# Layer norms turned by VectorE blocks and transfers instead of TensorE, in two graph attention layers

## The chip, the core and the metric

The kernel runs on one core of a Trainium2 chip. The metric is the device time of one execution in microseconds (us). The core's engines are called by the names of the profile: PE is TensorE (matmuls; PEld is its weight load, which overlaps), DVE is VectorE, ACT is ScalarE, POOL is GpSimd, and SP is SyncE, which here only issues transfers (DMAs). All data is float32.

## The reference

There are 64 graphs ("images" below) of 256 nodes with 512 features, x, and one 256 by 256 adjacency matrix. Two layers follow each other, both with a norm ahead and a residual behind:

```python
# layer 0: one head, additive attention
h = relu(layernorm(x))
h2 = h @ W                                  # 512 -> 256
e = leaky_relu(h2 @ a[0] + (h2 @ a[1]).T, 0.2) + NEG * (1 - adj)
x = x + concat([softmax(e) @ h2, h2], axis=-1)
# layer 1: eight heads of 64, masked dot-product attention
h = relu(layernorm(x))
q, k, v = (heads(h @ Wi.T + bi) for i in "qkv")
s = where(adj == 0, -inf, q @ k.T / 8)
x = x + merge(softmax(s) @ v) @ Wo.T + bo
```

A softmax without its maximum is exact as long as scores stay small. The kernel therefore bounds them from the weights' norms (the "bound check"), and at the end takes a second, slower program if the bound fails; with these inputs it does not.

## The kernel before, in words

The images are worked on in 32 groups of two (GB = 2, so GT = 4 tiles of 128 nodes each). Three groups are in flight at a time: while the attention of group g runs, the projections of group g + 1 and the first layer of group g + 2 are laid between its parts.

**The parts.** `first_layer(g)` is the whole of layer 0 and the norm of layer 1: statistics (line 340), rstd by a power on POOL (349), xn = (x - mean) * rstd on DVE (354), four 128 by 128 transposes per tile on PE into a PSUM bank pt (364), ReLU on ACT from the bank into hT (365), ph = hT by W0 (418), H copied by ACT (419), pn, the masked exponentials e, po = e by H (446), the new x and its statistics (450 to 454), and then the second norm with pt again. After it POOL makes `sums`, four sums and differences of quarters of hT (lines 376 to 379), and adds the output bias to x (470). The projections and the output product use a scheme of seven products of half-size blocks (`seven`, line 381), so that some products read hT itself and others a slice of sums: 1 and 2 read the first image's quarter of hT, 6 reads sums[1], 7 reads sums[2], 5 sums[0], 4 hT, 3 sums[3]. `project(g)` does the seven for q, k and v (21 pieces in the order 1, 2, 6, 7, 5, 4, 3), `outputs(g, b)` the seven for the output of one image, on o_sums, the same sums of oT.

**Attention.** `scores` makes sc for four heads (four PSUM banks), exponentials on ACT (572), the mask product p on DVE (573) and the sum ps on POOL (574). `weigh` of the step before makes pr (p by v) and total (line 601); DVE takes the reciprocal (604) and oT = pr * r (605).

**Order.** Everything on PE goes through `matmul` and `transpose` (lines 112 to 116, so nearly all of PE's work carries the lines 113 and 116), whose `in_order` ties each instruction to the one before it: PE's order is the program's. The other engines' orders come from the tile framework's scheduler. A group of attention has four steps; each is `weigh` of the step before, `scores`, and then pieces by a string written by hand:

```python
steps = ("uosuoosuosoosuos", "uusususususu", "uosoosuosoosuos", "uusususususu")
```

u is a piece of `project(g + 1)`, o of `outputs`, s of `first_layer(g + 2)` (which yields a GAP where it has nothing for PE). Where s finds nothing to do, a piece of the bound check, `judge()`, is run instead: it loads the weights once more in blocks of 128 columns, makes gram products and three squarings for q and k and four heads' pairs each (lines 267 to 292), and comes to a verdict.

**Buffers.** `mm` (line 90) hands out five PSUM banks in turn ("turn"): pr, sc, pt, ph, po, pn, the second bank of a projection and the second of an output product all come from it, so a bank's sixth user waits for the first one's reader. Three banks are held (`held_bank`). xn has two buffers, hT0 and hT1 two each.

**Transfers.** All are issued by SP in program order: x of group g + 3 in step two (line 125), the output of one image when its last add is done (654), the weights at the start (175, 186, 187), the check's blocks (247, 267).

**Start.** Group 0's first layer runs alone; after its second norm's first yield the constant bias b_out is made from bv by `last_bias` (lines 213 to 221: DVE makes a 128x128 tile bv, one buffer, PE multiplies, four times in turn), and the weights' sums by `weight_sums` on DVE.

Of the kernel before, what the change touches and what calls it, by code (L numbers as in the profile page):

```python
# [42 lines left out]
def bounded(  # L43
# [46 lines left out]
    def mm(name):  # L90
        return psum.tile([P, 512], F32, tag="turn", name=name, bufs=5)
# [117 lines left out]
    def last_bias():  # L209


        pb = mm("pb")
        for q in range(NQ):
            for half in range(2):
                b = small.tile([P, P], F32, tag="power", name=f"bv_{q}_{half}", bufs=1)
                nc.vector.tensor_scalar(b, ones, bv_col[:, half, q : q + 1], None, op0=ALU.mult)
                matmul(
                    pb, b, w_sb["o"][:, half, 2 * q : 2 * q + 2, :],
                    start=(q == 0 and half == 0), stop=(q == NQ - 1 and half == 1),
                )  # L220
        nc.vector.tensor_add(b_out, pb, b_out)


    def judge():
# [3 lines left out]

        part = const.tile([P, 10], F32, name="part")
        nc.vector.memset(part, 0.0)  # L230
        junk = att.tile([P, D], F32, tag="junk", name="junk", bufs=1)

        def squares(col, *srcs):
            sums = small.tile([P, HP], F32, tag="sums", name=f"sums{col}", bufs=2)
            for i, src in enumerate(srcs):
                nc.scalar.activation(
                    junk[:, : src.free_size()], src, AF.Square, accum_out=sums[:, i : i + 1]
                )
            nc.vector.reduce_sum(part[:, col : col + 1], sums[:, : len(srcs)], axis=AX.X)

        for s in range(2):
            squares(s, w0_sb[:, :, s])
        squares(2, *[w0_sb[:, c, 2:] for c in range(HP)])
        wv = att.tile([P, HP, D // HP], F32, tag="block", name="wv_block", bufs=1)
        sums = small.tile([P, HP], F32, tag="sums", name="sums3", bufs=2)
        for c in range(HP):
            nc.sync.dma_start(
                wv, wvT[:, c * P : (c + 1) * P].rearrange("(c p) o -> p c o", p=P)
            )
            nc.scalar.activation(  # L250
                junk, wv.rearrange("p c o -> p (c o)"), AF.Square, accum_out=sums[:, c : c + 1]
            )
        nc.vector.reduce_sum(part[:, 3:4], sums, axis=AX.X)
        squares(4, bcol["q"])
        squares(5, bcol["k"])
        squares(6, bv_col.rearrange("p h q -> p (h q)"))
        nc.vector.reduce_max(part[:, 7:8], bad.rearrange("p a t -> p (a t)"), axis=AX.X)
        yield
        heads = const.tile([P, P], F32, name="heads")
        nc.vector.memset(heads, 0.0)  # L260
        for j in range(2):
            nc.vector.memset(heads[j * DH : (j + 1) * DH, j * DH : (j + 1) * DH], 1.0)
        rowsq = const.tile([P, 2, HP], F32, name="rowsq")
        for n, (name, src) in enumerate((("q", wqT), ("k", wkT))):
            for hp in range(HP):
                w = att.tile([P, HP, P], F32, tag="block", name=f"w{name}_block{hp}", bufs=1)
                nc.sync.dma_start(
                    w, src[:, hp * P : (hp + 1) * P].rearrange("(c p) o -> p c o", p=P)
                )
                yield  # L270
                gram = mm(f"gram_{name}{hp}")[:, :P]
                for c in range(HP):
                    matmul(
                        gram, w[:, c, :], w[:, c, :], start=(c == 0), stop=(c == HP - 1)
                    )
                a = small.tile([P, P], F32, tag="power", name=f"power_{name}{hp}_0", bufs=1)
                nc.vector.tensor_mul(a, gram, heads)
                yield
                for i in range(3):
                    square = mm(f"square_{name}{hp}_{i}")[:, :P]  # L280
                    matmul(square, a, a, start=True, stop=True)
                    if i < 2:
                        a = small.tile(
                            [P, P], F32, tag="power", name=f"power_{name}{hp}_{i + 1}", bufs=1
                        )
                        nc.vector.tensor_copy(a, square)
                    else:
                        nc.scalar.activation(
                            junk[:, :P], square, AF.Square, accum_out=rowsq[:, n, hp : hp + 1]
                        )  # L290
                    yield
        nc.vector.reduce_sum(part[:, 8:10], rowsq, axis=AX.X)
        total = mm("total")[:, :10]
        matmul(total, ones, part, start=True, stop=True)
        norm = const.tile([P, 10], F32, name="norm")
# [44 lines left out]
        nc.vector.bn_stats(st, src[:, t, :])  # L340
        nc.vector.bn_aggr(mv[:, t, :], st)

    def norm_T(src, mv, name):


        ve = small.tile([P, GT], F32, tag="ve", name=f"ve{name}")
        nc.vector.tensor_scalar(ve, mv[:, :, 1], EPS, None, op0=ALU.add)
        rstd = small.tile([P, GT], F32, tag="rstd", name=f"rstd{name}")
        nc.gpsimd.tensor_tensor(rstd, ve, rexp, op=ALU.pow)
        xn = {}  # L350

        def normed(t):
            xn[t] = att.tile([P, D], F32, tag="xn", name=f"xn{name}_{t}", bufs=2)
            latest[0] = nc.vector.tensor_scalar(  # L354
                xn[t], src[:, t, :], mv[:, t, 0:1], rstd[:, t : t + 1],
                op0=ALU.subtract, op1=ALU.mult,
            ).ins.name

        def put(t, dst):
            if t + 1 < GT:  # L360
                normed(t + 1)
            pt = mm(f"pt{name}_{t}").rearrange("p (c t) -> p c t", c=HP)
            for c in range(HP):
                transpose(pt[:, c, :], xn[t][:, c * P : (c + 1) * P], ident)
            nc.scalar.activation(dst, pt, AF.Relu)  # L365

        normed(0)
        return put

    def halves(t, k):  # L370

        return [t[:, 2 * c : 2 * c + 2, r * k : (r + 1) * k] for r in range(2) for c in range(2)]

    def operand_sums(quads, sums):
        a11, a12, a21, a22 = quads
# [19 lines left out]

    def first_layer(g):

        xt = xs[g]
        mv = small.tile([P, GT, 2], F32, tag="mv", name=f"mv0_{g}")
        for t in range(GT):  # L400
            stats(mv, xt, t, f"0_{g}")
        put = norm_T(xt, mv, f"0_{g}")
        yield GAP

        H = big.tile([P, GT, F1 + 3], F32, tag="H", name=f"H_{g}", bufs=1)
        nc.gpsimd.memset(H[:, :, F1 + 2 :], 1.0)
        hT = {}
        for t in range(GT + 1):
            if t < GT:
                hT[t] = big.tile([P, HP, P], F32, tag="hT0", name=f"hT0_{g}_{t}")  # L410
                put(t, hT[t])
                yield
            if t == 0:
                continue
            t -= 1
            ph = mm(f"ph_{g}_{t}")[:, : F1 + 2]
            for c in range(HP):
                matmul(ph, hT[t][:, c, :], w0_sb[:, c, :], start=(c == 0), stop=(c == HP - 1))
            nc.scalar.copy(H[:, t, : F1 + 2], ph)  # L419
            nc.gpsimd.tensor_add(xt[:, t, F1:], H[:, t, 2 : F1 + 2], xt[:, t, F1:])  # L420
            yield

        pn = mm(f"pn_{g}")
# [17 lines left out]
        for r in range(GT):  # L441
# [11 lines left out]
            )  # L453
            stats(mv, xt, r, f"1_{g}")
            yield
        put = norm_T(xt, mv, f"1_{g}")
        yield GAP
        hT = big.tile([P, HP, TOK], F32, tag="hT1", name=f"hT1_{g}")
        for t in range(GT):
            put(t, hT[:, :, t * P : (t + 1) * P])  # L460
            if t == GT - 1:
                break
            yield
        sums = big.tile([P, 4, 2, N], F32, tag="sums", name=f"sums_{g}", bufs=1)
        quads = halves(hT, N)
        operand_sums(quads, sums)
        operands[g] = seven(quads, sums)

# [141 lines left out]

    def outputs(g, b):
        xt, oT = xs[g], oTs.pop((g, b))
        quads = halves(oT, P)
        sums = big.tile([P, 4, 2, P], F32, tag="o_sums", name=f"o_sums_{g}_{b}", bufs=1)
        operand_sums(quads, sums)
        ops = seven(quads, sums)
# [44 lines left out]
        for _ in part:  # L661
            pass

    gaps = 0
    for part in first_layer(0):
        gaps += part is GAP
        if part is GAP and gaps == 3:
            last_bias()
            weight_sums("q")
    short = first_layer(1) if NG > 1 else none  # L670
    for i, _ in enumerate(project(0)):
        if i % 7 == 1:
            weight_sums("kvo"[i // 7])
        next(short, None)
    run(short)
    verdict = judge()

    steps = ("uosuoosuosoosuos", "uusususususu", "uosoosuosoosuos", "uusususususu")
    waiting, late = None, none
    for g in range(NG):  # L680
        projected = project(g + 1) if g + 1 < NG else none
        short = first_layer(g + 2) if g + 2 < NG else none
        for step, parts in enumerate(steps):
# [8 lines left out]
            for part in parts:  # L692
                if part == "u":
                    next(projected, None)
                elif part == "o":
                    next(late, None)
                elif next(short, GAP) is GAP:
                    next(verdict, None)
        run(projected)
        run(short)  # L700
    weigh(*waiting)
    run(outputs(*waiting[:2]))
    run(verdict)


@with_exitstack
# [367 lines left out]
```

## Time and profile before

| what | us |
|---|---|
| median of 3 runs (lowest, highest) | 2699.2 (2699.19, 2699.45) |
| profiled execution: time | 2699.08 |
| profiled execution: span of the program on the core | 2697.3 |
| PE busy in the span | 2620.4 |
| DVE busy | 1669.7 |
| POOL busy | 1230.0 |
| ACT busy | 835.9 |
| PE, 4 transposes of a tile (pt) in the chain | 0.44 |
| DVE, xn 128x512, mean | 0.893 |
| ACT, ReLU from pt 128x512, mean | 0.599 |
| granted PE clock, mean over the run | 0.993 |

The profile is that of one execution. Its page gives busy shares, a chain of work followed back from the last instruction (who released whom), groups of instructions by line with their mean duration and the idle time of the engine ahead of them, and the transfers. The trace behind it can be asked for the instructions of an engine in order of time (timeline), for the same chain in a stretch (critical), and for busy times and the granted clock by stretches (windows). In a timeline a row is start, duration, engine, line, operation, names, and in brackets how long the engine sat idle before it and what ended that.

### The profile page before, as it was taken

What the parts mean: (1) busy time and instruction counts of PE and PEld (TensorE: products, weight loads), DVE (VectorE), ACT (ScalarE), POOL (GpSimd) and SP (SyncE); (2) the same over time, 40 slices, a digit from 0 to 9 for tenths busy, and PEclk for the clock granted to TensorE, in tenths of its full rate; (3) what the DMA queues carried; (4) which work ended last, traced back from release to release, by engine and by line L of the source; (5) the groups of instructions that cost most, each with busy time, mean ns of one, the idle gap of its engine ahead of it and who ended that gap; (6) DMA issues with size and microseconds to landing.
All of it is one profiled execution on the core that took longest, in us unless ns stands there. A gap on an engine that the chain in (4) does not pass through costs nothing.

```text
span 2697.3 us, 41512 instructions
## 1 busy us (share of the span) xinstructions
PE 2620.4 (97%) x17150; PEld 2118.8 (79%) x17150; DVE 1669.7 (62%) x2558; ACT 835.9 (31%) x1771; POOL 1230.0 (46%) x1004
## 2 busy tenths in 40 slices
PE   5999999999999999999999999999999999999997
PEld 3888888878888887887788888788878878878874
DVE  5666566666557665566665576665576656666544
ACT  2333232333332333323333323333333333233321
POOL 2353355443445443545434454435455335445343
PEclk8999999999999999999999999999999999999998
DMA  5000101000001010000000000000000000000000
GB/s 164 1 12 32 36 24 36 13 32 32 28 32 36 9 36 32 24 32 9 32 32 24 32 32 9 32 32 24 32 32 9 32 32 24 32 17 23 17 16 25
DMA packets 45890, 78.49 MB, mean 29 GB/s; under 512 B 3712, under 2 KB 10624, under 8 KB 45696
## 3 DMA queue, kind: packets, MB, share of 16 engines
q1 hardware_dynamic: 45696, 75.77, 8.1%
q8 instruction: 137, 2.24, 0.3%
q14 instruction: 57, 0.47, 0.1%
HBM read 42.21 MB, written 33.55 MB: 28 GB/s over the span
## 4 chain that ended last, share of the span: by engine, by line
PE 89%; DVE 8%; POOL 1%; issue 1%; DMA 0%; ACT 0%; DVEq 0%
PE pq L113 15%; PE pv L113 14%; PE py L113 13%; PE pk L113 13%; PE pr L113 9%; PE ph L113 8%; PE sc L113 7%; PE po L113 4%; PE pt L116 4%; DVE p L573 3%; DVE r L604 2%; PE total L113 2%; DVE k L544 1%; DVE oT L605 1%; PE pn L116 1%
## 5 line engine op out<-in xcount | busy, mean ns | idle before, releaser
L573 DVE TENSOR_TENSOR p<-p,maskT 128x1024 f32<-128x1024 f32 x256 | 398.6, 1588 | 0.6 <-ACT p L572 0.5
L572 ACT ACTIVATE p<-sc 128x512 f32<-128x512 f32 x512 | 264.4, 602 | 380.9 <-PE sc L113 380.9
L574 POOL TENSOR_TENSOR ps<-p 128x512 f32<-128x512 f32 x256 | 366.2, 1447 | 0.0
L628 DVE TENSOR_TENSOR x<-py,x 128x256 f32<-128x256 f32 x448 | 187.6, 419 | 272.8 <-PE py L113 266.9
L604 DVE RECIPROCAL r<-total 128x256 f32<-128x256 f32 x128 | 224.5, 1754 | 194.6 <-PE total L113 194.6
L113 PE MATMUL py<-wo_sb,o_sums 128*128 128x256 f32 x1024 | 266.5, 384 | 26.4 <-DVE x L628 21.6
L420 POOL TENSOR_TENSOR x<-H,x 128x256 f32<-128x256 f32 x128 | 87.7, 685 | 443.0 <-ACT H L419 441.9
L113 PE MATMUL pr<-p,v 128*32 128x256 f32 x4096 | 251.8, 385 | 5.8 <-DVE p L573 5.8
L113 PE MATMUL sc<-q,k 64*128 64x256 f32 x2048 | 255.7, 389 | 0.0
L113 PE MATMUL pq<-sums,wq_sb 128*128 128x256 f32 x1024 | 246.7, 384 | 4.2 <-POOL sums L377 3.7
L113 PE MATMUL ph<-w_sb,hT 128*128 128x258 f32 x1024 | 246.1, 383 | 0.0
L113 PE MATMUL pk<-sums,wk_sb 128*128 128x256 f32 x1024 | 244.8, 382 | 0.0
L113 PE MATMUL pv<-wv_sb,sums 128*128 128x256 f32 x1024 | 242.0, 379 | 0.1
L113 PEld LDWEIGHTS sc<-q,k 64*128 64x128 f32 x2048 | 187.2, 186 | 69.7 <-issue 52.6
L113 PEld LDWEIGHTS py<-wo_sb,o_sums 128*128 128x128 f32 x1024 | 191.2, 192 | 62.9 <-POOL o_sums L377 37.6
L365 ACT ACTIVATE hT<-pt 128x512 f32<-128x512 f32 x256 | 153.1, 599 | 266.0 <-PE pt L116 265.7
L354 DVE TENSOR_SCALAR xn<-x,mv,rstd 128x512 f32<-128x512 f32 x256 | 225.8, 893 | 9.5 <-PE pt L116 4.9
L376 POOL TENSOR_TENSOR o_sums<-oT 128x256 f32<-128x256 f32 x64 | 106.2, 1660 | 262.6 <-DVE oT L605 262.6
L113 PEld LDWEIGHTS pq<-sums,wq_sb 128*128 128x128 f32 x1024 | 190.1, 191 | 39.1 <-issue 9.9
L113 PEld LDWEIGHTS ph<-w_sb,hT 128*128 128x128 f32 x1024 | 195.7, 192 | 28.6
L113 PEld LDWEIGHTS pk<-sums,wk_sb 128*128 128x128 f32 x1024 | 189.3, 190 | 33.9 <-issue 9.9
L113 PEld LDWEIGHTS pr<-p,v 128*32 128x32 f32 x4096 | 121.1, 110 | 112.2 <-issue 39.7
(145 smaller groups left out, 4054.4 us busy)
## 6 DMA issues: line engine op xcount, KB each, us to landing
x<-in_x_dram SPq DMA_DIRECT2D x32, 1024.0 KB, 5.5
out_dram<-x SPq DMA_DIRECT2D x64, 512.0 KB, 2.8
wq_sb<-in_L_gnn_Wq_dram SPq DMA_DIRECT2D x2, 512.0 KB, 11.7
wk_sb<-in_L_gnn_Wk_dram SPq DMA_DIRECT2D x2, 512.0 KB, 12.4
wv_sb<-in_L_gnn_Wv_dram SPq DMA_DIRECT2D x2, 512.0 KB, 11.4
wo_sb<-in_L_gnn_Wo_dram SPq DMA_DIRECT2D x8, 128.0 KB, 3.3
wv_block<-in_L_gnn_Wv_dram SPq DMA_DIRECT2D x4, 256.0 KB, 3.0
wq_block<-in_L_gnn_Wq_dram SPq DMA_DIRECT2D x4, 256.0 KB, 2.9
```

Source lines behind the costliest of these rows:

```text
L113: in_order(nc.tensor.matmul(*args, **kwargs))
L116: in_order(nc.tensor.transpose(*args))
L354: latest[0] = nc.vector.tensor_scalar(xn[t], src[:, t, :], mv[:, t, 0:1], rstd[:, t : t + 1], op0=ALU.subtract, op1=ALU.mult,).ins.name
L365: nc.scalar.activation(dst, pt, AF.Relu)
L376: nc.gpsimd.tensor_add(sums[:, 0], a21, a22)
L420: nc.gpsimd.tensor_add(xt[:, t, F1:], H[:, t, 2 : F1 + 2], xt[:, t, F1:])
L544: nc.vector.tensor_add(part(1, 1), first, p7)
L572: nc.scalar.activation(pair[:, j], sc[j], AF.Exp, scale=scale)
L573: nc.vector.tensor_mul(pair, pair, maskT[:, None, :, :].to_broadcast([P, 2, NT, N]))
L574: nc.gpsimd.tensor_add(ps[:, 2 * i : 2 * i + 2, :], pair[:, :, 0, :], pair[:, :, 1, :])
L604: nc.vector.reciprocal(r, total)
L628: nc.vector.tensor_add(to, out, to)
```

## The change

For every group but the first (`by_pe` is false), a norm is no longer turned by PE. ACT applies the ReLU to xn in place; DVE's own transpose turns each tile in 32 by 32 blocks into xt, within the 32 partitions that a block lies in; and 16 transfers per image, each of 32 partitions and 256 pieces of 128 bytes, move the blocks from partitions 32i to partitions 32j of hT. xt has one buffer for all uses. hT0 is now one tile per image and not per 128 nodes, hT1 has the image as its outer dimension, and the pieces of `first_layer` are laid out anew: two tiles of xn, then an image turned and two more tiles, then the other image turned, two yields with nothing, then the products. Nineteen yields stand where there were twenty.

The bound check takes its gram products from the weights already in SBUF, four pairs of heads in one bank at a time, and runs in the pieces of group 0's first layer and projections; nothing of it is left in the main loop. The check's blocks are not loaded any more. `last_bias` makes its four bv tiles on POOL in one buffer of their own, without waiting for PE in between.

```diff
@@ last_bias
         pb = mm("pb")
+        b = att.tile([P, 2, 2, P], F32, tag="xt", name="bv_wide", bufs=1)
         for q in range(NQ):
             for half in range(2):
-                b = small.tile([P, P], F32, tag="power", name=f"bv_{q}_{half}", bufs=1)
-                nc.vector.tensor_scalar(b, ones, bv_col[:, half, q : q + 1], None, op0=ALU.mult)
+                nc.gpsimd.tensor_scalar(
+                    b[:, half, q, :], ones, bv_col[:, half, q : q + 1], None, op0=ALU.mult
+                )
...
@@ judge
+        for n, name in enumerate(("q", "k")):
+            gram = bank(f"gram_{name}")
+            for hp in range(HP):
+                half, cols = hp // 2, slice(hp % 2 * P, (hp % 2 + 1) * P)
+                for c in range(HP):
+                    w = w_sb[name][:, c % 2, c // 2 * 2 + half, cols]
+                    matmul(gram[:, hp, :], w, w, start=(c == 0), stop=(c == HP - 1))
...
+        for i in range(3):
+            for n, name in enumerate(("q", "k")):
+                square = bank(f"square_{name}{i}")
+                for hp in range(HP):
+                    a = power[name][:, hp, :]
+                    matmul(square[:, hp, :], a, a, start=True, stop=True)
...
@@ norm_T
-    def norm_T(src, mv, name):
+    def norm_T(src, mv, name, by_pe):
...
             ).ins.name
-
-        def put(t, dst):
-            if t + 1 < GT:
-                normed(t + 1)
-            pt = mm(f"pt{name}_{t}").rearrange("p (c t) -> p c t", c=HP)
-            for c in range(HP):
-                transpose(pt[:, c, :], xn[t][:, c * P : (c + 1) * P], ident)
-            nc.scalar.activation(dst, pt, AF.Relu)
...
+            if not by_pe:
+                nc.scalar.activation(xn[t], xn[t], AF.Relu)
+
+        def turned(b, dst):
+            if by_pe:
...
+                return
+
+            J = P // S
+            xt = att.tile([P, J, HP, NT, S], F32, tag="xt", name=f"xt{name}_{b}", bufs=1)
+            for t in range(NT):
+                nc.vector.transpose(
+                    xt[:, :, :, t, :], xn[b * NT + t].rearrange("p (c j a) -> p j c a", c=HP, a=S)
+                )
+            for i in range(J):
+                for j in range(J):
+                    to = dst[j * S : (j + 1) * S, :, :].rearrange("a c (t i n) -> a c t i n", t=NT, n=S)
+                    nc.sync.dma_start(
+                        to[:, :, :, i, :], xt[i * S : (i + 1) * S, j]
+                    )
...
@@ first_layer
+        by_pe = g == 0
...
+        hT = [big.tile([P, HP, N], F32, tag="hT0", name=f"hT0_{g}_{b}") for b in range(GB)]
+        normed(0)
+        normed(1)
+        yield GAP
+        turned(0, hT[0])
+        normed(2)
+        normed(3)
+        yield GAP
+        turned(1, hT[1])
+        yield GAP
+        yield GAP
+        for r in range(GT):
+            b, t = divmod(r, NT)
+            ph = mm(f"ph_{g}_{r}")[:, : F1 + 2]
...
-        put = norm_T(xt, mv, f"1_{g}")
+        normed, turned = norm_T(xt, mv, f"1_{g}", by_pe)
+        normed(0)
+        normed(1)
         yield GAP
-        hT = big.tile([P, HP, TOK], F32, tag="hT1", name=f"hT1_{g}")
-        for t in range(GT):
-            put(t, hT[:, :, t * P : (t + 1) * P])
-            if t == GT - 1:
-                break
-            yield
+        hT = big.tile([P, GB, HP, N], F32, tag="hT1", name=f"hT1_{g}")
+        turned(0, hT[:, 0])
+        normed(2)
+        normed(3)
+        yield GAP
+        turned(1, hT[:, 1])
+        yield GAP
+        yield GAP
         sums = big.tile([P, 4, 2, N], F32, tag="sums", name=f"sums_{g}", bufs=1)
...
@@ bounded, the start
-    gaps = 0
-    for part in first_layer(0):
-        gaps += part is GAP
-        if part is GAP and gaps == 3:
+    verdict = judge()
+    for piece, _ in enumerate(first_layer(0)):
+        if piece == 8:
+            next(verdict)
+        if piece == 13:
             last_bias()
+            next(verdict)
+        if piece == 15:
             weight_sums("q")
...
         next(short, None)
+        next(verdict, None)
+    run(verdict)
     run(short)
-    verdict = judge()
...
@@ bounded, the loop
-                elif next(short, GAP) is GAP:
-                    next(verdict, None)
+                else:
+                    next(short, None)
```

In the changed kernel's own numbering the ReLU is line 355, DVE's transpose 370, the transfers 376, the sums 384 to 387, the reciprocal 623 and oT 624.

## The prediction

> **What bounds the kernel now.** I read the page first: busy shares, then the chain that ended last.
>
> ```profile
> span 2697.3 us, 41512 instructions
> ...
> PE 2620.4 (97%) x17150; PEld 2118.8 (79%) x17150; DVE 1669.7 (62%) x2558; ACT 835.9 (31%) x1771; POOL 1230.0 (46%) x1004
> ...
> PE 89%; DVE 8%; POOL 1%; issue 1%; DMA 0%; ACT 0%; DVEq 0%
> ```
>
> TensorE is the bound: only 77 us of the span is without it. So a matmul removed shortens the run, and a wait put in front of one lengthens it by its full size, for line 105 (in_order) fixes TensorE's order by hand. The chain of two steps in the middle of the run gives the size of both.
>
> ```profile
> 1073.97 1.86 PE pr L113 x32
> 1075.84 0.43 PE total L113 x8
> 1076.27 1.93 PE sc L113 x16
> ...
> 1083.80 0.44 PE pt L116 x4
> ...
> 1098.61 0.86 PE py L113 x4
> 1099.47 1.73 PE pq L113 x8
> ```
>
> The columns are start, length, what. A step opens with pr, total and sc (4.22 us); then come projection products (1.73), output products (0.86) and, as pt, the norm's transposes: 0.44 us per tile. The pr of 1010.4 and 1092.5 open the same step of two groups: a group takes 82 us.
>
> **What is removed.** Each of groups 1 to 31 loses 8 tiles of pt: 8 x 0.44 = 3.5 us of TensorE per group. The bound check's 32 gram products and 24 squares, two passes each at 0.11 us (square_k: two passes in 0.22), leave the main loop: 112 x 0.11 = 12 us.
>
> **What is added.** Per tile a 32 by 32 transpose on VectorE (T), behind a ReLU on ScalarE that before read PSUM (0.60, hidden: ScalarE is 31% busy). Per image 16 transfers on SP, in a row; one buffer xt, so the next image's T waits for all 16. No row shows T. Nearest are VectorE's one-input 128x512 instructions: 0.41 (line 151) below, and 1.75 above, the reciprocal (line 604), the slowest pass. I take 0.69, what copy, reduction and statistics of that shape take.
>
> The page "VectorE: DVE Perf Modes" of the Trainium skill (The three transpose paths) gives VectorE 311 ns for 128x128 in bf16, by estimate 1.24 us for T, and its rules send a full 128x128 transpose to TensorE; no run here shows T yet. With 1.24 the sum below would rise by 33 us.
>
> For the transfers, SP's own rows at the start, 32 partitions each:
>
> ```profile
> 25.04 0.43 SPq L186 DMA_DIRECT2D wo_sb<-in_L_gnn_Wo_dram  x1
> 25.51 0.42 SPq L187 DMA_DIRECT2D bv_col<-in_L_gnn_bv_dram  x1
> ```
>
> The pitch is 0.47 us and small ones land 2.2 to 2.4 us after issue, so a set of 16 takes 15 x 0.47 + 2.3 = 9.4 us. Bounds: 0.35 and 2.2 give 7.5; 0.55 and wo_sb's 3.3 give 11.6 (the pitch of 1.36 before 24 us belongs to waits for 512 KB transfers). Pieces of 128 bytes should not bind: the 1,024 four-byte pieces of the q and k biases ran in about 1.5 us, so 256 need 0.4.
>
> The page "DMA: Bandwidth & Descriptors" (Rules for kernel authors) says that transfers under 64 KB pay mostly overhead and should be merged; its fit for GpSimd's transfers (Anatomy of one DMA), 2.0 us plus bytes over 436 GB/s, would make 16 of 32 KB one by one 33 us. The rows above overlap them instead.
>
> **First new wait: last step of a group, 1.9 us.** The order of the changed kernel's instructions shows what stands on VectorE ahead of oT (line 605), which frees pr's bank; five banks turn, pr and four sc take all, and the second v product takes pr's. Count from the step's pr. The last po ends at -2.6 (a projection and an output product now follow it). Then ri, x, three statistics and the small ones 3.2 (rows from 1074.01 on), to 0.6; rstd on POOL 1.0; xn 0.55, xn beside POOL 1.2, statistics 0.66: 4.1. T, reciprocal 1.75, T, oT 0.69 end at 7.9. The product was due at 4.22 + 1.92 = 6.1 (before, oT ended at 5.2): it waits until 8.0. The step is then 8.0 + 6 x 1.73 = 18.4 long. T at 0.41 makes the wait 1.3; T at 1.75 makes it 4.0.
>
> **Second new wait: next group's first step, 5.8 us.** The third q product needs sums (line 377). Before, POOL made sums ahead of o_sums:
>
> ```profile
> 1092.61 1.28 POOL L376 TENSOR_TENSOR sums<-hT 128x512 f32<-128x512 f32 x1 [1.41 <-PE pv L113]
> ...
> 1095.08 1.27 POOL L377 TENSOR_TENSOR sums<-sums,hT 128x512 f32<-128x512 f32 x1
> ...
> 1097.66 1.70 POOL L376 TENSOR_TENSOR o_sums<-oT 128x256 f32<-128x256 f32 x1
> ...
> 1101.80 2.50 POOL L574 TENSOR_TENSOR ps<-p 128x512 f32<-128x512 f32 x2
> ```
>
> After, POOL's order is o_sums (three), ps (two), then sums in the order 376, 378, 377. On VectorE: reciprocal 2.35 to 4.1, xn 0.55, oT to 5.4. On POOL, by the groups' means: 1.66 + 1.58 + 0.73, 2 x 1.45, 1.28 + 1.30 + 1.31 = 10.7, so line 377 is done at 16.2. TensorE is there at 4.22 + 1.92 + 0.86 + 1.73 + 1.73 = 10.4. Wait: 5.8.
>
> Are the transfers later than POOL? The last step's first image: T done at 7.2, landed 16.6. Its second image's T stands behind the sixth v product's add (17.4): done 18.8, landed 28.2, which is 9.8 in the next step; POOL comes to it at 12.3. Hidden, with 2.5 us to spare. The next group's first image: T after the third py add, 12.3, landed 21.7; ph is due at 24.8. Second image: landed 36.4, due 37.9. So at 9.4 us per set no transfer is waited for in the loop; from 11 on it is.
>
> **Third: the clock.** This trace has the same wait once, at the start:
>
> ```profile
> 63.66 3.40 PE L113 MATMUL pq<-sums,wq_sb 128*128 128x256 f32 x8 [3.69 <-POOL sums L377]
> ...
> 67.33 1.89 PE L113 MATMUL pq<-sums,wq_sb 128*128 128x256 f32 x8
> ```
>
> After 3.7 us of idling, the granted clock from 63.2 to 66.4 was 0.50, and the product took 3.40, where the next took 1.89 (1.73 in the chain, which leaves out the overlap of neighbours). A wait of 2.17 us (to 105.75) had full speed behind it. So the 5.8 us wait costs 1.7 more; the 1.9 us one does not.
>
> **Sum.** Per group 1.9 + 5.8 + 1.7 - 3.5 = 5.9 us. The step pair stands 30 times (groups 2 to 31 are prepared in the loop): +177. The check: -12. The start: bv on POOL lets pb follow po at once, not after 8.5 us and three more waits for VectorE: about -10; group 1's pt -3.5; its transfers lie beside little work: about 4 us before each image's ph, and from its last po to its first sums some 31 us (two sets 18.8, T and statistics 8, sums 4) over 18 us of products, 13 of wait: together +7. The profiled execution took 2699.1 (span 2697.3 and 1.8 around it), the median of the runs is 2699.2: 2699 + 177 - 12 + 7 = 2871; I forecast 2870. Costed at nothing: VectorE's added 8 T per group (5.5 us of 82, at 62% busy), covered except where counted; were TensorE never to wait, nothing of it would show.
>
> **Rivals.** (a) The transfers and POOL hide after all: only -3.5 per group, -105 - 12 + 7, 2590. For it: POOL is idle over half the time. Against: POOL's order, and a wait of 3.7 us in all per group already eats the gain. (b) Transfers set the pace: with 12 us per set, T waits for the set ahead of it, sums are ready at 18.1 and the fourth set 1.1 late: +3.0 per group, 2960; with 16 us every T holds VectorE up, about 29 per group, over 3500. It decides from 11 us per set. For it: 2,000 transfers of 128-byte runs, SBUF to SBUF, of which there is no row. (c) T costs 1.75: the first wait becomes 4.0, over the idling (3.1 to 3.7) that halved the clock in this trace: +3.8 per group, 2985. (d) Slower than the point of balance only by a little: POOL's chain runs shorter and the clock holds, 2.5 per group less, 2795.
>
> **Chances.** Forecast with its neighbours (2790 to 2940) 0.60, (b) 0.16, (c) 0.12, (a) 0.08, between (a) and no change 0.04. Range 2760 to 3010: it takes in T from 0.41 (2853) to 1.75 (2985), a set from 7.5 (2870) to 11.6 (2950), and (d); left out are (a) and the far part of (b). Measurement tells 0.2% (5 us) from no change: faster 0.09, same 0.03, slower 0.88.
>
> **What would show it.** In the profile after: about 250 us of idle TensorE instead of 77, most of it before pq<-sums with POOL sums as releaser, some 60 before pv with VectorE's oT; half clock in every group; T near 0.7; hT's transfers landing within 2.5 us of issue. The forecast is wrong if pq<-sums does not wait, if ph waits for a DMA, or if T is over 1.2.

## The result, and the profile after

The changed kernel takes 2985.0 us (median of 4 runs, 2980.3 to 2987.3) against 2699.3 for the kernel before (4 runs, 2699.2 to 2699.5): the ratio is 1.106, with a 95% interval of 1.104 to 1.108. The direction was forecast, and the range of 2760 to 3010 holds the time. The forecast itself, 2870, is 115 us short: 171 us more were expected, 286 came.

First the page of the changed kernel: span, busy shares, the chain that ended last by engine, then the one row of the transfers (KB each, us from issue to landing).

```profile
span 2985.7 us, 42596 instructions
...
PE 2625.0 (88%) x16158; PEld 2071.3 (69%) x16158; DVE 1822.7 (61%) x2783; ACT 842.8 (28%) x1759; POOL 1237.0 (41%) x1008
...
PE 49%; SPq 23%; DVE 13%; DMA 5%; POOL 4%; issue 4%; ACT 1%; DVEq 0%; POOLq 0%; ACTq 0%
...
hT<-xt SPq DMA_DIRECT2D x1984, 32.0 KB, 2.0
```

TensorE is busy for about as long as before although 992 matmul rows are gone, and it is now idle for 361 us of the span and not 77 (the rows of pq, ph, pv and py that stand behind waits took longer; see the clock below). In the chain, SP's queue (SPq) and the transfers (DMA) hold 28%, where DMA had 0% and SPq no entry. Below is who TensorE waits for (us in all, times, longest). pq, pk and pv are the projection products of q, k and v, py is the output product, and kept_v is ScalarE's copy of a v product out of its bank, behind which the next product adds to that bank:

```profile
PE pq L113 <- POOL sums L385: 207.7, 31, 13.6
PE pv L113 <- ACT kept_v L533: 58.4, 29, 2.3
PE ph L113 <- DMA hT<-xt: 23.6, 22, 5.8
...
PE pq L113 <- DMA hT<-xt: 4.8, 1, 4.8
```

The two waits that were forecast are there, 6.5 us per group before the third q product (207.7 less the start's 13.6, over 30) and 2.0 before a v product. A third one, ph for a transfer, was not to come. The cause of the smaller one is not the forecast's either: pv waits for kept_v, a copy on ScalarE, and not for VectorE's oT.

One group's rows in the timeline show how they hang together (start, length, engine, line, what; in brackets the idle time and what ended it). The last step of the group opens with pr at 1113.73, the next group's first with pr at 1132.51.

```profile
1119.83 37.92 SPq L376 DMA_DIRECT2D hT<-xt  x48
...
1124.57 0.63 ACT L355 ACTIVATE xn<-xn 128x512 f32<-128x512 f32 x1 [3.99 <-DVE xn L350]
...
1125.97 0.63 ACT L355 ACTIVATE xn<-xn 128x512 f32<-128x512 f32 x1 [0.78 <-DVE xn L350]
1126.51 1.05 ACT L533 COPY kept_v<-pv 128x512 f32<-128x512 f32 x2
...
1127.13 1.99 PE L113 MATMUL pv<-wv_sb,sums 128*128 128x256 f32 x8 [2.00 <-ACT kept_v L533]
...
1132.70 1.30 DVE L370 STREAM_TRANSPOSE xt<-xn 128x512 f32<-128x512 f32 x2 [1.12 <-DMA hT<-xt]
...
1141.82 2.49 POOL L593 TENSOR_TENSOR ps<-p 128x512 f32<-128x512 f32 x2
...
1145.99 1.30 DVE L370 STREAM_TRANSPOSE xt<-xn 128x512 f32<-128x512 f32 x2 [2.49 <-DMA hT<-xt]
1146.02 1.27 POOL L384 TENSOR_TENSOR sums<-hT 128x512 f32<-128x512 f32 x1 [1.71 <-DMA hT<-xt]
...
1149.97 3.77 PE L113 MATMUL pq<-sums,wq_sb 128*128 128x256 f32 x8 [6.93 <-POOL sums L385]
```

SP is taken by three sets in a row from 1119.83 to 1157.75, each held up only by the landing of the one before and the T behind it: the second image's T (1132.70) waits for the first set, the next group's T (1145.99) for the second. The second set runs from T's end, 1134.00, to 1145.99: **12.0 us**. POOL is through with ps at 1144.31 and then waits 1.7 us more, for that set. ScalarE's row shows the smaller wait: kept_v stands behind two ReLUs that wait for xn.

The granted clock around it (us, PE busy, PEld, DVE, ACT, POOL, PEclk, DMA share, GB/s):

```profile
1142.90:1149.90 7.00, 0.14 (x1) 0.00 (x0) 4.33 (x5) 0.63 (x1) 5.29 (x5) 0.78 0.19 29
1149.90:1153.40 3.50, 3.43 (x8) 2.80 (x9) 0.30 (x1) 0.63 (x1) 1.34 (x2) 0.50 0.35 54
```

The clock falls to half within the idle 7 us and stays there for the whole product behind it: 3.77 us where the next one took 1.89.

### The profile page after: what moved, and what is told of

It reads as the page before. It is cut to its first block, busy times and chain, and to the rows that moved or that the text cites. A ratio compares the mean times of both kernels' runs of the same rounds, so it can differ in the third digit from the quotient of the medians.

```text
span 2985.7 us, 42596 instructions
## 1 busy us (share of the span) xinstructions
PE 2625.0 (88%) x16158; PEld 2071.3 (69%) x16158; DVE 1822.7 (61%) x2783; ACT 842.8 (28%) x1759; POOL 1237.0 (41%) x1008
## 4 chain that ended last, share of the span: by engine, by line
PE 49%; SPq 23%; DVE 13%; DMA 5%; POOL 4%; issue 4%; ACT 1%; DVEq 0%; POOLq 0%; ACTq 0%
SPq L376 23%; PE pk L113 11%; PE py L113 9%; PE pq L113 8%; PE ph L113 7%; DMA hT<-xt 5%; PE pr L113 4%; PE po L113 4%; PE sc L113 3%; DVE xt L370 3%; DVE st L335 3%; DVE r L623 2%; DVE xn L350 2%; PE pv L113 2%; POOL rstd L345 1%
## 5 line engine op out<-in xcount | busy, mean ns | idle before, releaser
L113 PE MATMUL pq<-sums,wq_sb 128*128 128x256 f32 x1024 | 303.0, 448 | 210.3 <-POOL sums L385 207.7
L113 PEld LDWEIGHTS pq<-sums,wq_sb 128*128 128x128 f32 x1024 | 223.0, 224 | 269.1 <-POOL sums L385 222.3
L593 POOL TENSOR_TENSOR ps<-p 128x512 f32<-128x512 f32 x256 | 388.1, 1536 | 2.9 <-DVE p L592 2.9
L592 DVE TENSOR_TENSOR p<-p,maskT 128x1024 f32<-128x1024 f32 x256 | 368.0, 1469 | 2.8 <-ACT p L591 2.7
L384 POOL TENSOR_TENSOR o_sums<-oT 128x256 f32<-128x256 f32 x64 | 103.8, 1623 | 582.0 <-DVE oT L624 582.0
L355 ACT ACTIVATE xn<-xn 128x512 f32<-128x512 f32 x248 | 152.6, 628 | 539.5 <-DVE xn L350 537.4
L113 PE MATMUL pv<-wv_sb,sums 128*128 128x256 f32 x1024 | 246.5, 390 | 60.6 <-ACT kept_v L533 58.4
L113 PE MATMUL ph<-w_sb,hT 128*128 128x258 f32 x1024 | 253.2, 391 | 38.6 <-DMA hT<-xt 23.6
L113 PE MATMUL py<-wo_sb,o_sums 128*128 128x256 f32 x1024 | 278.3, 403 | 5.1 <-POOL o_sums L385 4.2
L113 PEld LDWEIGHTS pv<-wv_sb,sums 128*128 128x128 f32 x1024 | 195.5, 193 | 98.8 <-ACT kept_v L533 70.0
L350 DVE TENSOR_SCALAR xn<-x,mv,rstd 128x512 f32<-128x512 f32 x256 | 244.5, 985 | 24.3 <-POOL rstd L345 23.5
L113 PEld LDWEIGHTS py<-wo_sb,o_sums 128*128 128x128 f32 x1024 | 209.0, 207 | 51.0 <-issue 10.6
L370 DVE STREAM_TRANSPOSE xt<-xn 128x512 f32<-128x512 f32 x248 | 163.2, 686 | 108.7 <-DMA hT<-xt 107.6
```

The source lines that it names most:

```text
L113: in_order(nc.tensor.matmul(*args, **kwargs))
L350: latest[0] = nc.vector.tensor_scalar(xn[t], src[:, t, :], mv[:, t, 0:1], rstd[:, t : t + 1], op0=ALU.subtract, op1=ALU.mult,).ins.name
L355: nc.scalar.activation(xn[t], xn[t], AF.Relu)
L370: nc.vector.transpose(xt[:, :, :, t, :], xn[b * NT + t].rearrange("p (c j a) -> p j c a", c=HP, a=S))
L384: nc.gpsimd.tensor_add(sums[:, 0], a21, a22)
L592: nc.vector.tensor_mul(pair, pair, maskT[:, None, :, :].to_broadcast([P, 2, NT, N]))
```

## The experiments

All kernels below are the changed kernel with the edit shown. "First pr" is the loop's first pr, one step into it (before: 127.0), "group" the mean distance of the groups' first pr over the first 29 groups (before: 82.0, of which some 0.5 is the check's products), "sums" the median time from the pr of a group's last step to the first of the next group's sums on POOL; all three are worked out from the traces.

| kernel | us | ratio to before (95%) | first pr | group | sums |
|---|---|---|---|---|---|
| changed kernel | 2985.0 | 1.106 (1.104 to 1.108) | 168.5 | 90.2 | 32.5 |
| pe_norms | 2673.9 | 0.991 (0.989 to 0.992) | 136.1 | 80.8 | |
| layer0_blocks | 2654.1 | 0.983 (0.982 to 0.985) | 148.4 | 79.7 | |
| layer1_blocks | 2944.7 | 1.092 (1.090 to 1.093) | 154.6 | 89.2 | 32.4 |
| two_queues | 2849.8 | 1.056 (1.054 to 1.058) | 146.0 | 86.4 | 23.8 |
| sums_first | 3111.8 | 1.153 (1.151 to 1.154) | 168.1 | 94.3 | 32.2 |
| runs_1k | 2920.8 | 1.082 (1.080 to 1.083) | 158.5 | 88.4 | 26.2 |
| four_transfers | 2681.9 | 0.994 (0.992 to 0.995) | 140.4 | 81.0 | 20.6 |
| relu_on_dve | 3085.5 | 1.142 (1.139 to 1.144) | 171.6 | 93.6 | |
| relu_after_kept | 2987.3 | 1.106 (1.104 to 1.108) | 170.0 | 90.3 | 32.4 |
| four_relu | 2691.8 | 0.997 (0.996 to 0.998) | 138.4 | 81.3 | |
| layer0_late | 2646.7 | 0.980 (0.979 to 0.981) | 138.8 | 79.8 | |
| three_sets | 2716.0 | 1.006 (1.005 to 1.007) | 137.1 | 82.3 | |

### Which norm, and what is left without blocks

pe_norms:

```diff
-        by_pe = g == 0
+        by_pe = True
```

> All norms are turned by TensorE again; the new layout of pieces, the bound check in the first group and bv on POOL stay. Theory 1 (the whole loss comes from the blocks and their transfers; the check's products are moved, not removed, and what leaves the main loop, 12 us, is paid at the start): 2699 - 13 + 12, so 2690 to 2705, with the first pr at 137 to 142 us instead of 127.0. Theory 2 (the forecast's own costing: the products cost nothing at the start, and pb follows po at once): 2699 - 12 - 10 = 2677. Theory 3 (the new layout of pieces itself costs): above 2715.

layer0_blocks gives True to layer 1's `norm_T`, layer1_blocks to layer 0's:

```diff
-        normed, turned = norm_T(xt, mv, f"1_{g}", by_pe)
+        normed, turned = norm_T(xt, mv, f"1_{g}", True)
```

> Blocks in layer 0's norm alone, layer 1's norm on TensorE. Theory 1 (the wait belongs to layer 1's second set, which sums wait for; two sets of 12.4 us per group lie well inside 82 us): no pq<-sums wait in the loop, four pt of 0.44 us saved in each of 31 groups, 55 us less than the kernel with all norms on TensorE, so 2640 to 2660, with some 10 us of ph waits at the start. Theory 2 (the load of 4 T on VectorE, 4 ReLU on ScalarE and 32 transfers slows the group wherever it is put): about half of the loss stays, 2800 to 2850.

> Blocks in layer 1's norm alone, layer 0's norm on TensorE. Theory 1 (the wait before pq<-sums, 6.9 us and a half-speed product, belongs to layer 1's two sets alone): it stays as it is, ph no longer waits, 1.76 us of pt come back per group: 2960 to 3010. Theory 2 (the four sets of a group queue up on SP behind each other, so that half as many sets wait much less): the wait falls below 3.5 us and the time to 2800 to 2870.

pe_norms took 2674, below what theory 1 gave and close to the forecast's own costing, but not for the forecast's reasons: its start is 9 us longer, not 10 shorter, and a group is 0.7 us shorter than before's later groups (81.5), which neither the forecast nor the three theories had. Before, TensorE waited 21.6 us in 27 output products for VectorE's x; with the new layout that wait is down to 0.8. So the new layout, with the check and bv moved, is worth 25 us of gain; the whole loss, 311 us against pe_norms, is the blocks'.

Layer 0's blocks gain: 2654, 20 less than pe_norms though their start is 12 us longer. Layer 1's alone take 2945, somewhat below theory 1's 2960: the wait before pq<-sums stays (188.6 us in 31 times). The loss belongs to layer 1's norm: its blocks alone cost 271 us against pe_norms, layer 0's alone gain 20, and both together cost 311. So some 60 us come only when both are there; three sets in a row on SP and ph's waits in the loop are seen in that case alone.

### POOL's order, or the transfers?

The forecast laid the large wait to POOL's order (o_sums and ps ahead of sums); the rows above suggest that the transfers were no earlier. sums_first turns POOL's order round:

```diff
...
+        of = operand_sums(quads, sums)
+        if b == GB - 1:
+            for o_sum in (of[0], of[2]):
+                after(o_sum, made[0])
```

Here made[0] is the last of the next group's four sums, and the two o_sums of the second image that read oT alone are put behind it.

> POOL is made to take the next group's four sums ahead of o_sums and ps, all else as in the changed kernel. Theory 1 (the transfers set the pace: the second set lands 13.5 us after the step's pr, sums are done at 17.4 whatever stands ahead of them): the sums come no earlier, o_sums come after them, at about 22, and the output product that stands before the third q product on TensorE waits for them: about 5 us more per group, 3100 to 3170. Theory 2 (the forecast's: POOL's order makes the wait, since o_sums and ps stand ahead of sums for 7.6 us): 2 to 5 us less per group, 2830 to 2920.

Theory 1 holds, with 3112 us. The waits of TensorE in this kernel:

```profile
PE py L113 <- POOL o_sums L386: 352.6, 32, 12.6
...
PE pq L113 <- POOL sums L386: 12.8, 1, 12.8
```

The sums began 32.2 us after the last step's pr, in the changed kernel 32.5: with POOL's o_sums and ps out of their way they came no sooner. Only o_sums came later, and the output product took over the wait.

two_queues lets ScalarE issue every second transfer:

```diff
-                    nc.sync.dma_start(
+                    (nc.sync, nc.scalar)[j % 2].dma_start(
```

> The 16 transfers of a set are issued half by SP and half by ScalarE, the rest as in the changed kernel. Theory 1 (SP's pitch of 0.655 us sets the pace of a set): a set takes about 7.5 us instead of 12.4, T no longer waits for the set before, POOL starts sums when ps is done, 1.7 us earlier, ph does not wait, the start is 10 to 15 us shorter: 2880 to 2920. Theory 2 (the data movement of 128-byte pieces sets the pace): a set stays at 12 us and the time at 2975 to 2995. Theory 3 (the eight issues on ScalarE stand in front of exponentials and copies): ACT p or kept becomes a releaser of waits of TensorE and the time is above 2990.

2850 us is a larger gain than theory 1 gave. A set takes 7.5 us from its first issue to its last landing, where it took 11.8 (medians), sums come 8.7 us sooner, the start is 22 us shorter. TensorE's waits here:

```profile
PE py L113 <- POOL o_sums L385: 68.4, 18, 5.0
PE pv L113 <- ACT kept_v L533: 60.4, 58, 2.9
...
PE pq L113 <- POOL sums L385: 7.3, 1, 7.3
```

The wait before pq<-sums is gone but for the start. The median pitch of both queues is 0.66 us, so what was halved is issuing, not moving. POOL's order changed with it, sums now ahead of o_sums, which by itself (sums_first) had made the kernel slower. No run has short sets and the changed kernel's order on POOL, so what the short sets would gain without the new order is not shown. The Trainium skill, page "DMA: Bandwidth & Descriptors" (Rules for kernel authors), says that spreading transfers over several engines does not help bandwidth and only saves the issuing engine's time; the run agrees, and here that time, with POOL's new order, was worth 135 us. Theory 3 was partly right too: kept_v and copies on ScalarE stand behind the issues, and 60 us of waiting for kept_v are left.

### What a transfer costs SP

runs_1k writes each partition's kilobyte as one run, four_transfers moves a set in 4 transfers of 128 KB:

```diff
# runs_1k
...
+                    to = dst[j * S : (j + 1) * S, :, :].rearrange("a c n -> a (c n)")
+                    run = HP * NT * S
...
+                    nc.sync.dma_start(
+                        to[:, i * run : (i + 1) * run],
+                        xt[i * S : (i + 1) * S, j].rearrange("a c t n -> a (c t n)"),
+                    )
...
# four_transfers
...
+                nc.sync.dma_start(
+                    dst[i * S : (i + 1) * S, :, :].rearrange("a c n -> a (c n)"),
+                    xt[i * S : (i + 1) * S].rearrange("a j c t n -> a (j c t n)"),
+                )
```

> The same 16 transfers of 32 KB per set, from the same partitions to the same partitions, but each partition's kilobyte is written as one run and not as eight of 128 bytes; the blocks then stand at other columns of hT than the products read them from, so the output isn't the reference's. The scheduler lays ps between the sums on POOL here. Theory 1 (an issue costs SP the same whatever it describes): pitch 0.65 us, a set 12.4, 2970 to 3000. Theory 2 (the cost grows with the 256 runs of a transfer): pitch 0.47 or less as in the rows of the weights, a set at 9.5 or less, the wait before pq<-sums shorter by 3 us or more, 2860 to 2920.

> The same bytes of a set in 4 transfers of 128 KB, from 32 partitions to the same 32 partitions, one run of 4 KB per partition; the blocks are not moved across partitions, so the output isn't the reference's. POOL's order here has sums ahead of o_sums. Theory 1 (SP's pitch times the number of transfers is the set's time): a set 3 x 0.65 + 3 = 5 us, no wait before pq<-sums of over 1 us and none of ph in the loop, the two waits of 3.5 us per group and the half clock gone, 2640 to 2700. Theory 2 (what a set moves sets its time): a set above 10 us and a time above 2900. Theory 3 (T, the ReLU and the new order cost by themselves): sets short but the time above 2750.

The median issue is 0.609 us with 256 runs of 128 bytes, 0.589 with 32 runs of a kilobyte, and 0.589 with 32 runs of 4 KB and four times the bytes; with the gap behind it, 0.653, 0.633 and 0.634. In these three shapes an issue from SBUF to SBUF costs SP 0.6 us, whatever it describes. That the memories make the difference from the forecast's rows is not shown: in the changed kernel a load of x out of DRAM, issued 0.04 us behind a set (at 269.73), took 0.60 too, and 0.39 in two_queues, where SP had been idle before it (at 237.68). For the pitch theory 1 holds; for the time of runs_1k neither does: 2921 us lies between the two, at the edge of theory 2's range. The scheduler gave POOL another order in it, part of the sums ahead of o_sums, and sums began at 26.2; so of this run only the pitch is used.

With four transfers the waits for transfers are gone but for the start. In its rows for T and for the transfers T sits idle 3.0 us in all, where it was 108.7:

```profile
L370 DVE STREAM_TRANSPOSE xt<-xn 128x512 f32<-128x512 f32 x248 | 163.7, 679 | 3.0 <-DMA hT<-xt 2.9
```

```profile
hT<-xt SPq DMA_DIRECT2D x496, 128.0 KB, 2.4
```

The same bytes in a quarter of the issues take 2682 and not 2985; POOL's new order and the runs of 4 KB are part of that step, and the moves across partitions are left out. That is the page's rule on small transfers (same page and section: merge what is under 64 KB), which the forecast had weighed and set aside; the 33 us for a set that it worked out from the page's fit were too dear (12.0 measured), the rule's direction was right.

### The smaller wait

relu_on_dve moves the ReLU to VectorE:

```diff
-                nc.scalar.activation(xn[t], xn[t], AF.Relu)
+                nc.vector.tensor_scalar_max(xn[t], xn[t], 0.0)
```

> The ReLU of a tile runs on VectorE instead of ScalarE, all else as in the changed kernel. Theory 1 (the wait of 2.0 us before pv<-sums comes from ScalarE, where two ReLUs that wait for VectorE stand ahead of kept_v; and SP's three sets in a row set the end): that wait falls below 0.7 us, the wait before pq<-sums grows by as much, 2970 to 3000. Theory 2 (the forecast's: the bank is freed late by oT, behind T on VectorE): the wait before pv grows by 0.5 to 1 us, 2990 to 3030. Theory 3 (each wait adds on its own): 2985 - 29 x 2, 2925 to 2940.

3085 us lies above all three theories. The ReLU took 1.2 us a tile on VectorE, and the last v product then waited 146.8 us in 31 times for VectorE's own v. It shows that VectorE has no room for 1.2 us more per tile in that step, and leaves the question open. relu_after_kept asks it without adding work:

```diff
-            if not by_pe:
+            if not by_pe and not (name[0] == "1" and t >= NT):
...
+                if name[0] == "1" and b == 1:
+                    relu = nc.scalar.activation(xn[b * NT + t], xn[b * NT + t], AF.Relu)
+                    if kept_v[0]:
+                        after(relu, kept_v[0])
...
+                    kept_v[0] = nc.scalar.copy(to, bank).ins.name
```

> In layer 1's norm the ReLUs of the second image's two tiles are put behind the copy kept_v of the third v product on ScalarE (before, they stood ahead of it, waiting for xn from VectorE); the rest as in the changed kernel. Theory 1 (these two ReLUs make the 2.0 us wait before pv<-sums; and the three sets in a row, which begin with the first image's T, set when sums are ready): the wait before pv falls below 0.5 us, the one before pq<-sums grows from 6.6 to about 8.5 us, the time stays at 2970 to 3000. Theory 2 (each wait adds on its own): the wait before pv falls, the other stays, 2985 - 30 x 2 to 2.5, 2910 to 2930. Theory 3 (the forecast's: oT behind T frees the bank late): the wait before pv stays near 2 us.

Theory 1 holds in both halves. Groups of TensorE (busy, mean ns, idle before and its releaser), first in the changed kernel, then in this one:

```profile
L113 PE MATMUL pq<-sums,wq_sb 128*128 128x256 f32 x1024 | 303.0, 448 | 210.3 <-POOL sums L385 207.7
...
L113 PE MATMUL pv<-wv_sb,sums 128*128 128x256 f32 x1024 | 246.5, 390 | 60.6 <-ACT kept_v L533 58.4
```

```profile
L113 PE MATMUL pq<-sums,wq_sb 128*128 128x256 f32 x1024 | 303.6, 449 | 262.3 <-POOL sums L389 259.6
...
L113 PE MATMUL pv<-wv_sb,sums 128*128 128x256 f32 x1024 | 233.1, 381 | 2.2 <-DVE v L568 2.2
```

The wait before pv<-sums fell from 60.6 to 2.2 us (8.2 us of waiting for kept_v came up before pv<-hT, 0.3 each), the wait before pq<-sums rose from 210.3 to 262.3, and the time is unchanged. The two are not two costs that add up: the second ends when the transfers end, 32.4 us after the last step's pr, however TensorE spends the time until then.

> The 4 transfers of 128 KB per set that move no block across partitions (the output isn't the reference's), and the order of the ReLUs of relu_after_kept. Without the transfers' wait, removing the wait of 2.0 us before pv<-sums should now count in full: 2682 - 30 x 2.0 to 2.7 (its half clock too), 2600 to 2625. If instead it moves on to another wait as in the changed kernel, the time stays above 2665.

four_relu is four_transfers with that same order, and no faster: 2692, so the wait moved on, the second of the two cases. kept_v's wait fell from 58.0 to 8.4 us, but 57.8 us came up before the last v product, for VectorE's v. In one group's timeline the add that frees that bank (VectorE's v, 1174.49) stands behind two T and two xn, which begin at 1172.35. So even without transfers' waits VectorE's queue holds that step; whether another order there would free it was not tried.

### A version that beats both

```diff
-        by_pe = g == 0
+        by_pe = g <= 1
...
-        normed, turned = norm_T(xt, mv, f"1_{g}", by_pe)
+        normed, turned = norm_T(xt, mv, f"1_{g}", True)
```

> Blocks in layer 0's norm alone and from group 2 on; group 1's norms, which lie at the start beside little work, are on TensorE like group 0's. Theory 1 (the start's extra 12.3 us of the kernel with layer 0's blocks belong to group 1's transfers; the loop's gain stays): 2654 - 12, 2638 to 2646, faster than both kernels. If the 12 us come from something else at the start: 2650 to 2658.

2646.7, 0.7 us above theory 1's range (lowest run 2640.6) and 2.0% faster than before (interval 1.9 to 2.2). Of the 53 us some 25 are already in pe_norms; the blocks of layer 0 give the other 27, 1.0%. Most of layer0_blocks' extra start is gone: first pr at 138.8 and not 148.4. ph waits for transfers 2.6 us in all and pq for none; TensorE is at 97% again:

```profile
PE 2575.9 (97%) x16670; PEld 2063.0 (78%) x16670; DVE 1680.8 (64%) x2655; ACT 834.7 (32%) x1759; POOL 1239.6 (47%) x1008
```

three_sets has the first image of layer 1 turned by blocks as well (`by_pe` as a list per image: `[g <= 1, g <= 1]` in layer 0, `[g <= 1, True]` in layer 1).

> As layer0_late, and the first image of layer 1's norm turned by blocks too, the second by TensorE: three sets per group. Theory 1 (what hurts in layer 1 is the second set, queued behind the first; the first alone lands some 18 us after the last step's pr, about when the next step begins): two more pt per group saved, 0.88 x 30 = 26 us less than layer0_late if sums are in time, 2612 to 2622; at most 1 us per group of wait before pq<-sums, so up to 2645. If a single set in front of sums is already too late, a wait of 3 us or more and its half clock come back: above 2740.

2716 us is neither case. The sums are in time (pq<-sums idles 0.7 us in all), so a single set is not too late. But the step that prepares it is 2.5 us longer, for pt now waits for xn, and a v product for kept_v:

```profile
1177.66 0.63 PE L116 MATMUL pt<-ident,xn 128*128 128x128 f32 x4 [1.21 <-DVE xn L350]
1178.98 0.66 PE L116 MATMUL pt<-ident,xn 128*128 128x128 f32 x4 [0.69 <-DVE xn L350]
...
1184.76 1.99 PE L113 MATMUL pv<-wv_sb,hT 128*128 128x256 f32 x8 [1.67 <-ACT kept_v L533]
```

The first wait is for VectorE's queue. The second is that of the changed kernel: in ScalarE's rows kept_v (1184.14) stands behind two ReLUs (1183.08) that waited for xn. The order of relu_after_kept was not tried here.

## Why the prediction was right in direction and short in size

Per group (the groups after the check's, 81.5 us, against 90.2 now: +8.7 measured, +5.9 forecast) and for the start:

| step | forecast | measured |
|---|---|---|
| pt removed, per group | -3.5 | -3.5 (its rows are gone; not measured alone) |
| T | 0.69 us | 0.686 |
| a set of 16 transfers | 9.4 (7.5 to 11.6) | 12.0 in the row shown, 11.8 in the median |
| first new wait | 1.9 | 2.0 |
| second new wait | 5.8 | 6.5 |
| ph's waits | 0 | 0.9 (0.4 put down to transfers) |
| half clock | 1.7 | 3.0 |
| new layout of pieces | 0 | -0.7 |
| check, once | -12 | -13 in the loop, +14 at the start |
| start without the check | +7 | +27 (41.5 less 14) |

The rows per group sum to +8.2 of the 8.7 measured, with the -3.5 taken as it was forecast (in layer0_blocks, where half of the pt are gone, a group is 1.1 us shorter than in pe_norms and not 1.8). (0.9 is ph's 38.6 us less the start's 11.4, over 30; 3.0 is what the matmuls of unchanged count take longer than in pe_norms, 93 us over 31 groups.)

**The transfers were the mis-sized term, and it changed the cause.** The forecast took SP's pitch of 0.47 us from small transfers out of DRAM at the start; in the sets it is 0.65. So 15 x 0.653 + 2.0 makes 11.8, where 9.4 was taken and 11.6 was the high bound. The sentence "Hidden, with 2.5 us to spare" is where it failed: with 12.0 per set the second image's T, which waits for the first set, ended 20.3 us after pr and not 18.8, its set landed at 32.3 and not 28.2, and that was 1.7 us after POOL was free. The forecast's own rival (b) had this case, "it decides from 11 us per set", and at 12 us it gave 2960, much nearer to the time; I had put 0.16 on it and 0.60 on the set that hides. POOL's order was a true constraint, 1.7 us behind the one that bound, and so the wait's size (5.8 against 6.5) looked right under the wrong name; that was luck. sums_first shows that POOL's order is not what bound; that it would have made the forecast's 5.8 us had the sets been short is not shown. Rival (c) had the measured time, 2985, for a T of 1.75 us; T took 0.686, so that agreement is chance. One thing in the chain stayed untried: a second buffer for xt would let the second set follow without waiting for the first to land (by estimate 31 x 0.653 + 2.0 = 22.2 us after 1119.83, at 1142.1, ahead of POOL's 1144.31).

**The first wait** had its size by luck and not its cause: no row shows a wait for oT's bank (oT ended 6.5 us after pr, not 7.9), and TensorE waited for kept_v behind the ReLUs on ScalarE. "hidden: ScalarE is 31% busy" was the step at fault: what counted was not ScalarE's share but what its queue held in front of kept_v, two instructions that waited for VectorE. That it costs nothing on top while the transfers bind (relu_after_kept) was not foreseen either.

**The half clock** came in every group, as forecast, but at 3.0 us: the estimate was read from one product, and others run at half speed too (py<-wo_sb,o_sums 403 ns and not the 387 of pe_norms, pv<-wv_sb,sums 390 and not 379).

**The start** is 41.5 us longer where +7 was forecast, and that bv on POOL "lets pb follow po at once" failed: the new bv tiles stand on POOL behind the power of group 1's first norm. POOL in pe_norms:

```profile
43.14 1.01 POOL L345 TENSOR_TENSOR rstd<-ve,rexp 128x4 f32<-128x4 f32 x1 [2.21 <-DVE ve L343]
44.14 2.35 POOL L216 TENSOR_SCALAR bv_wide<-ones,bv_col 128x128 f32<-128x128 f32 x4
```

TensorE waited 9.4 us for them, before 8.5 and three short ones. The check's products leave the loop, but they are not gone: TensorE runs them for 14 us at the start, which the forecast left out of the sum. Before the first pr TensorE is busy 103.8 us in pe_norms, where it was 93.1 before, and idle 1.5 us less; that makes pe_norms' +9. Group 1's transfers beside little work make the rest: +12.3 for layer 0 and +18.5 for layer 1, each put in alone, 30.8 of the 32.4 us by which the changed kernel's first pr stands behind pe_norms'. (in_order, which the forecast puts at line 105, stands at line 107.)

**Right were** T (the estimate of 1.24 us, worked out from the figure in "VectorE: DVE Perf Modes", The three transpose paths, is not what this shape in float32 took: 0.686), the shape of the loss (two waits and a half clock in every group, most of it before pq<-sums), and the direction. Of the three signs that were to tell it wrong, one came true: ph waits for a DMA.

## What to carry to other kernels

Count a chain of small transfers by its issues: number times the issuing queue's pitch, plus one landing, with the pitch read from a run of like transfers where there is one (0.47 us from the start's small loads was too short here); then ask of every buffer in the chain who waits for the whole set. When two chains end near each other at a wait, name both and their distance, since the share of busy time, or a releaser, names only the last: here turning POOL's order round made the kernel slower, and taking ScalarE's queue out of the way gained nothing. Work that leaves the critical engine was worth taking where its result is due late (layer 0's blocks: 27 us or 1.0% less than with all norms on TensorE) and not where it is due at once (layer 1's: 271 us or 10% more).

## What the runs showed of the hardware

- The issue of a transfer from SBUF to SBUF took SP 0.59 to 0.61 us whether it had 256 runs of 128 bytes, 32 of 1 KB or 32 of 4 KB; ScalarE's queue took 0.62. SP's small issues out of DRAM at the start took 0.31 to 0.51, a load of x alone 0.39 and behind a set 0.60. Why was not tried.
- Two queues at once hardly slowed each other at 32 KB per transfer: the median pitch was 0.66 us on both against 0.65 on one, landing 2.0 us after issue; only the second issue of a set on SP was clearly longer, 0.81 us against 0.61.
- VectorE's transpose of 128x512 in float32 took 0.69 us, as long as its copy of that shape (maskT<-pt_mask, 0.68, one instruction of the kernel before).
- Behind the waits of 5.3 to 7.8 us before pq<-sums the product took 3.4 to 3.8 us in every group, where it takes 1.9 at full speed. Of the 30 waits of 2.0 to 2.3 us before pv<-sums 8 had a slower product behind them (2.6 to 3.2 us where 2.0 is usual; a step of 20.5 us where it is 18.8 in most).
